# A Perceiver block on one core: key unit between first scores and values, feed-forward by two batches, self-attention norms batch by batch

## The chip, the core and the metric

The kernel runs on one core of one Trainium2 chip. The core has five engines with instruction streams of their own: TensorE (PE, matrix products), VectorE (DVE), ScalarE (ACT), GpSimd (POOL) and SyncE (SP, which issues most transfers). ACT and POOL issue transfers as well. [...] The metric is the device time of one execution in microseconds; the time of the kernel before is the median of three runs.

## What is computed

The block takes `x` (8 batches of 128 rows of 512) and a context (8 batches of 2048 rows of 384). All of it is float32, except where the feed-forward rounds.

```python
# 1. cross-attention over the context, 8 heads of 64
q = layernorm(x) @ Wq;  k = context @ Wk;  v = context @ Wv
x = x + softmax(q k^T / 8) v @ Wo + bo
# 2. masked self-attention; its input is n = layernorm(x)
n = layernorm(x)
logits = (n Wq + bq)(n Wk + bk)^T, -inf above the diagonal
x = x + n + (softmax(logits, axis=1) / sqrt(512)) @ (n Wv + bv)
# 3. feed-forward, 2048 hidden columns; n = layernorm(x)
h = quantize_e4m3(relu(n @ w1.T + b1))
x = x + quantize_e5m10(h @ quantize_e4m3(w2).T + quantize_e5m10(b2))
```

`layernorm` has no scale and no shift. `quantize` rounds to a small float format; the kernel does it with five DVE instructions.

## The kernel before, in words

**Order of the work.** The order on PE is that of the program text from beginning to end (`manual_schedule` of PE). The order on ACT and DVE is also that of the text, until the first quarter of the last batch is done (`in_turn.close()`, `first.close()`); from there a scheduler orders them by what is ready. POOL and SP are ordered by the scheduler throughout. Seven of the eight PSUM banks are handed round under the tag `bank`; the eighth holds the attention output `po`.

**Cross-attention.** For each batch b and each quarter m (two heads), the main loop (L721 to L780) issues, in this order on PE: `scores(b, m)` (16 products, L476), `attend` of the quarter before (64 products, L521), and a *unit* that prepares later data: `v_proj(b, 1)` in m = 0, `v_proj(b+1, 0)` in m = 1, `k_proj(b+1, m-2)` in m = 2 and 3. For the last batch the units are the self-attention's projections of rows 0 to 3. Between parts of the unit the other engines do the softmax of the quarter: DVE takes the maxes while copying the scores to `p` (L480, L486, L488), ACT takes the exponentials in two halves (`exps`, L494), DVE turns 32 x 32 blocks in place (`turns`, L507), and SP stores sixteen pieces of `p` into `pT` (L510), which `attend` of the next quarter reads. `p` and `pT` have one buffer each, so a quarter's maxes can start only when the quarter before has landed in `pT`.

**Units.** `k_proj` and `v_proj` use `block_product`: twenty products of sums of blocks in place of twenty-four, into seven banks, with `take` (a copy on ACT, L300) and `with_bank` or `less_bank` (additions on DVE, L303, L306) between. A bank that PE writes again must have been read before. The sums of the context's blocks are made by POOL (`sum_half`, L205), for the first batch by DVE. A unit is a generator: `first_of` issues it up to its next `yield` (after the first `take`, and after the fifth), `all_of` issues the rest. The first key unit is a plain product (`k_plain`, L353 to L366) over half the context; the other half of batch 0's keys is `k_proj(0, f2, (1,))`.

**Start.** `EARLY` products of an identity run before the first data are there. Then follow `k_plain(0)`, `q_norm(0)`, `k_plain(1)`, the transposes of the normed queries (`q_turn`), the query projection (`q_proj`), whose result goes to DRAM and is read back per batch (`load_q`), `k_proj(0, 0, (1,))`, `v_proj(0, 0)`, and `k_proj(0, 1, (1,))` before the loop. A one-element Exp (`warm`) makes ACT load its Exp table.

**Between cross-attention and self-attention.** In m = 0 of batch b, the output of batch b-1 is normalized and projected (`project`, L559 to L564: eight products, an addition on DVE into `xs[b]`, and for b up to 5 a store of the rows to DRAM, `xr`, from SP). In m = 0 of the last batch `bring_rows` (L566) reads rows 0 to 5 back, POOL issuing; `enter_self_attention` loads the three weights `swq`, `swk`, `swv` on POOL's queue; and rows 0 to 3 are normed and turned: statistics and subtraction on DVE (L111 to L118), Sqrt on ACT (L115), four transposes on PE (L131), a copy on ACT (L132), and `xs = xs + xn` on POOL (L124), each for one row block of 128. Rows 4 to 6 are normed by `sa1.norm` before the last `attend`, and turned after the last `project`; row 7 is normed and turned last.

**Feed-forward.** `hidden` (L824 to L838) makes the hidden columns for four batches at once: a product has 512 columns of four batches; two blocks of 128 hidden columns are rounded together. `output` (L841) has 16 products for one batch, `finish` (L849) adds the bias, rounds, adds the rows on POOL and stores. The last four batches' outputs stand behind the last hidden block.

Of the kernel before, what the change touches and what calls it, by code (L numbers as in the profile page):

```python
# [17 lines left out]
P = 128  # L18
# [29 lines left out]
def tile_perceiver_block(  # L48
# [34 lines left out]
    NG = 2  # L83
    TMPB = 2
    BK = 256
    EARLY = 9
    GB = B // NG
    GT = GB * S
    RSK = float(D) ** -0.5
# [264 lines left out]
    def k_plain(f2):  # L354


        k_tile(0, f2)
        pss = {(j, n): bank(f"k_{f2}_{j}_{n}") for j in range(2) for n in range(2)}
        for n, k in ((0, 0), (0, 1), (0, 2), (1, 0), (1, 1), (1, 2)):
            for j in range(2):  # L360
                nc.tensor.matmul(  # L361
                    pss[j, n], wk4[:, k, f2, j, :], xraw[0, 0][:, k, 2 * n : 2 * n + 2],
                    start=(k == 0), stop=(k == NKC - 1),
                )
        for (j, n), ps in pss.items():
            nc.scalar.copy(kts[0, f2][:, j, ts(n, 512)], ps)  # L366

    def k_proj(b, f2, halves=(0, 1)):

# [182 lines left out]
    def load_x(b):  # L552
        xs[b] = xp.tile([P, D], F32, tag="x", name=f"x_{b}")
        nc.sync.dma_start(xs[b], xd[:, b, :])

    def project(b, ot):
# [27 lines left out]
    class SelfAttention:  # L584


        def __init__(self, g, pool, w):
            self.g, self.pool = g, pool
            self.swq, self.swk, self.swv, self.bq, self.bk, self.bv, self.mask = w
            self.rows = [g * GB + i for i in range(GB)]  # L590
            self.xt = pool.tile([P, NK, GT], F32, tag="xt", name=f"xt_{g}")
            self.xn, self.es, self.vals = {}, {}, None

        def norm(self, b):
# [17 lines left out]
                    yield  # L612

        def queries(self):
            all_of(self.turned_rows("q", self.swq, self.bq))

        def keys(self):
            all_of(self.turned_rows("k", self.swk, self.bk))

        def weights(self, b):  # L620

            i = b % GB
            ps = bank(f"pl_{b}")
            for k in range(NK):
                nc.tensor.matmul(
                    ps[:, :S], self.kt[:, k, ts(i, S)], self.qt[:, k, ts(i, S)],
                    start=(k == 0), stop=(k == NK - 1),
                )
            lg = self.pool.tile([P, S], F32, tag="lg", name=f"lg_{b}", bufs=2)
            nc.vector.tensor_tensor(lg, ps[:, :S], self.mask, ALU.add)  # L630
            nm = small.tile([P, 1], F32, tag="snm", name=f"snm_{b}", bufs=4)
            nc.vector.reduce_max(nm, lg, axis=AX.X, negate=True)
            e = self.pool.tile([P, S], F32, tag="e", name=f"e_{b}", bufs=4)
            den = small.tile([P, 1], F32, tag="sden", name=f"sden_{b}", bufs=4)
            nc.scalar.activation(e, lg, AF.Exp, bias=nm, accum_out=den)
            r = small.tile([P, 1], F32, tag="sr", name=f"sr_{b}", bufs=4)
            nc.vector.reciprocal(r, den)
            nc.vector.tensor_scalar(e, e, r, RSK, ALU.mult, ALU.mult)
            self.es[b] = e

        def values(self, b):
            if self.vals is None:

                self.vals = self.pool.tile([P, GB, D], F32, tag="sk", name=f"sv_{self.g}")
            ps = bank(f"psv_{b}")
            for k in range(NK):
                nc.tensor.matmul(  # L647
                    ps, self.xt[:, k, ts(b % GB, S)], self.swv[:, k, :],
                    start=(k == 0), stop=(k == NK - 1),
                )  # L650
            nc.vector.tensor_tensor(self.vals[:, b % GB, :], ps, self.bv, ALU.add)

        def read(self, b):
            ps = bank(f"pr_{b}")
# [17 lines left out]
    def enter_self_attention():  # L672
        src.close()
        wsa = ctx.enter_context(tc.tile_pool(name="wsa", bufs=1, reuse_waits="tile"))
        sap = ctx.enter_context(tc.tile_pool(name="sap", bufs=1, reuse_waits="tile"))
        w = [
            load_w(wsa, a, NK, n, nc.gpsimd)
            for a, n in ((sa_wq, "swq"), (sa_wk, "swk"), (sa_wv, "swv"))
        ]
        w += [load_columns(wsa, sa_bq, "bq"), load_columns(wsa, sa_bk, "bk")]  # L680
        w.append(load_row(wsa, sa_bv, "bv"))

        mask = wsa.tile([P, P], F32, tag="mask", name="mask")
# [6 lines left out]
        return sap, w  # L690
# [25 lines left out]

# [4 lines left out]
    for b in range(B):  # L721
        last = b + 1 == B
        for m in range(NK):
# [11 lines left out]
            elif not last:  # L735
                unit = k_proj(b + 1, m - 2)
            elif m == 1:
                unit = sa0.turned_rows("q", sa0.swq, sa0.bq)
            elif m == 2:
                unit = sa0.turned_rows("k", sa0.swk, sa0.bk)  # L740
            else:
                for r in sa0.rows:
                    sa0.weights(r)
            if b == m == 0:

                first_of(unit)
                first_of(unit)
            exps(b, m, 0)
            if unit and not b == m == 0:
                first_of(unit)  # L750
            exps(b, m, 1)
            if m == 0 and b > 0:
                turned = normalized_first(b - 1)
                if last:
# [10 lines left out]
            if m == 0:  # L765
# [24 lines left out]
    xa.close()  # L790
    project(B - 1, ot)
    sa1.norm(sa1.rows[-1])
    for r in sa1.rows[:-1]:
        sa1.turn(r)
    for r in sa0.rows[2:]:
        sa0.read(r)
    sa1.turn(sa1.rows[-1])
# [21 lines left out]
            turned_into(xt, b, normed(b, sap, "xn", GB, "f"), "f")  # L819
        return xt  # L820

    hqs = {}

    def hidden(g, xt, blocks):  # L824
        if g not in hqs:
            hqs[g] = tp.tile([P, NHC, GT], BF16, tag="hq", name=f"hq_{g}", bufs=2)
        for c in blocks:
            h = tp.tile([P, 2, GT], F32, tag="h", name=f"h_{g}_{c}")
            for i in range(2):
                ps = bank(f"ph_{g}_{c + i}")  # L830
# [5 lines left out]
                nc.scalar.activation(  # L836
                    h[:, i, :], ps, AF.Relu, bias=b1c[:, c + i : c + i + 1]
                )  # L838
            quantize(nc, tp, hqs[g][:, c : c + 2, :], h, E4M3, "qh")

    def output(b, ps, blocks, cols=slice(0, D)):  # L841
        g, i = b // GB, b % GB
        for c in blocks:
            nc.tensor.matmul(  # L844
                ps[:, cols], hqs[g][:, c, ts(i, S)], w2[:, c, cols],
                start=(c == 0), stop=(c == NHC - 1),
            )

# [32 lines left out]
    for i in range(2):  # L881
# [58 lines left out]
```

## Time and profile before

| what | us |
|---|---|
| median of three runs | 1136.22 |
| lowest and highest run | 1134.65, 1136.40 |
| profiled execution, its time | 1134.23 |
| profiled execution, its span | 1132.5 |
| mean granted TensorE clock in it | 0.994 of full speed |
| DVE, ACT and POOL busy | 825.2, 329.4, 232.0 |

The profile is of one execution. "Busy" is the time in which an engine had an instruction under way. A line such as `PE pq L444 <- ACT xq L132: 1.0, 1, 1.0` in the list of waits says that PE, with the instruction of line 444 that writes tile `pq`, sat for 1.0 us until ACT had finished line 132's `xq`, once, the longest time 1.0. In the chain that ended last, each row has a start, a length, the engine, the tile, the line, and the number of instructions (x16). In a timeline row, the text behind the arrow `<-` of tile names tells what an instruction reads, and the bracket tells how long the engine idled before it and what ended that. `PEld` is the loading of weights, which runs beside PE. `SPq`, `ACTq` and `POOLq` are the issuing of transfers on an engine's queue. A stretch of the table by stretches gives start and end, their difference, then busy time and number of instructions of PE, PEld, DVE, ACT and POOL.

### The profile page before, as it was taken

Reading aid. Unit: us, or ns where it says so; the run is one execution under the profiler, and the core shown is the slowest. Engines: PE = TensorE matmul, PEld = TensorE weight load, DVE = VectorE, ACT = ScalarE, POOL = GpSimd, SP = SyncE. Lnnn points to the kernel's source line nnn. Section 1 sums busy time; section 2 is a strip of 40 time slices with the busy share of each in tenths; the row PEclk is TensorE's granted clock in tenths of the full one; section 3 lists DMA queues with packets and bytes.
Section 4 is the critical chain, followed back from the end, with each engine's and each line's share of the span. In section 5 each row is a group of like instructions: output and inputs, shape, how many; then the busy total and the mean of one; then the engine's idle time right before and its main releaser. Section 6 shows DMA issues by size and latency. Waiting matters only on the chain.

```text
span 1132.5 us, 16240 instructions
## 1 busy us (share of the span) xinstructions
PE 1110.0 (98%) x6034; PEld 787.3 (70%) x6034; DVE 825.2 (73%) x1705; ACT 329.4 (29%) x499; POOL 232.0 (20%) x322
## 2 busy tenths in 40 slices
PE   9999999999999999999999999999999999999996
PEld 5486787778878887777888788877865544444443
DVE  4946777676767776777777768767795559766867
ACT  3233222223323322222333232222342322222010
POOL 0304400540251044005303600440030000000101
PEclk9999999999999999999999999999999999999998
DMA  8412644643554465455335544653393473000001
GB/s 287 170 54 65 164 103 99 166 104 85 130 149 91 108 152 145 94 127 153 85 84 143 137 102 104 149 141 75 81 264 75 94 248 106 9 0 1 28 9 38
DMA packets 48495, 125.09 MB, mean 110 GB/s; under 512 B 10384, under 2 KB 15520, under 8 KB 47520
## 3 DMA queue, kind: packets, MB, share of 16 engines
q1 hardware_dynamic: 46192, 117.48, 40.1%
q0 software_dynamic: 1360, 5.78, 1.7%
q8 instruction: 48, 0.79, 0.3%
q10 hardware_dynamic: 864, 0.79, 0.2%
q14 instruction: 31, 0.25, 0.1%
HBM read 49.03 MB, written 7.86 MB: 50 GB/s over the span
## 4 chain that ended last, share of the span: by engine, by line
PE 94%; DVE 3%; DMA 2%; ACT 1%; issue 0%; SPq 0%; POOL 0%; DVEq 0%; ACTq 0%; POOLq 0%
PE pv_z L400 20%; PE pk_z L377 19%; PE po L521 10%; PE sc L476 10%; PE ph L832 10%; PE pk_b L377 3%; PE pv_b L400 3%; PE psq L606 2%; PE pq L444 2%; PE psk L606 2%; PE psv L647 2%; PE pf L844 2%; PE py L559 2%; PE k L361 2%; DMA pT<-p 2%; DVE p L507 1%
## 5 line engine op out<-in xcount | busy, mean ns | idle before, releaser
L494 ACT ACTIVATE p<-p,nm 128x2048 f32<-128x2048 f32 x64 | 128.1, 2002 | 430.9 <-DVE nm L488 331.1
L507 DVE STREAM_TRANSPOSE p<-p 128x512 f32<-128x512 f32 x256 | 158.9, 679 | 85.1 <-ACT p L494 84.9
L480 DVE TENSOR_SCALAR_CACHE_REDUCE p<-sc 128x512 f32<-128x512 f32 x256 | 159.0, 686 | 30.5 <-PE sc L476 28.8
L400 PE MATMUL pv_z<-wv_sums,x 128*128 128x256 f32 x640 | 158.9, 383 | 0.8 <-ACT v L300 0.8
L205 POOL TENSOR_TENSOR m<-x 128x256 f32<-128x256 f32 x70 | 51.3, 733 | 521.7 <-DMA x<-in_ctx_t_dram 458.5
L377 PE MATMUL pk_z<-x,wk_sums 128*128 128x256 f32 x600 | 149.4, 382 | 0.4 <-DVE kt L306 0.4
L400 PEld LDWEIGHTS pv_z<-wv_sums,x 128*128 128x128 f32 x640 | 121.0, 191 | 20.5 <-issue 1.9
L521 PEld LDWEIGHTS po<-pT,v 128*64 128x64 f32 x2048 | 112.8, 138 | 24.3 <-issue 22.0
L377 PEld LDWEIGHTS pk_z<-x,wk_sums 128*128 128x128 f32 x600 | 112.7, 190 | 18.5 <-issue 2.9
L476 PE MATMUL sc<-kt,q 64*128 64x512 f32 x512 | 119.6, 602 | 2.5 <-DVE p L480 2.5
L521 PE MATMUL po<-pT,v 128*64 128x128 f32 x2048 | 120.5, 276 | 0.0
L400 PE MATMUL pv_z<-wv_sums,m 128*128 128x256 f32 x448 | 108.6, 382 | 2.6 <-DVE v L303 2.4
L832 PE MATMUL ph<-xf,w 128*128 128x512 f32 x256 | 110.4, 592 | 0.0
L377 PE MATMUL pk_z<-m,wk_sums 128*128 128x256 f32 x420 | 101.9, 380 | 0.7 <-ACT kt L300 0.7
L400 PEld LDWEIGHTS pv_z<-wv_sums,m 128*128 128x128 f32 x448 | 83.6, 191 | 16.1 <-DVE v L303 2.8
L832 PEld LDWEIGHTS ph<-xf,w 128*128 128x128 f32 x256 | 48.6, 190 | 60.4 <-issue 59.8
L476 PEld LDWEIGHTS sc<-kt,q 64*128 64x128 f32 x512 | 47.3, 186 | 62.2 <-issue 53.5
L377 PEld LDWEIGHTS pk_z<-m,wk_sums 128*128 128x128 f32 x420 | 78.9, 190 | 13.2 <-ACT kt L300 1.1
L300 ACT COPY v<-pv_z 128x512 f32<-128x512 f32 x112 | 62.8, 589 | 60.6 <-PE pv_z L400 60.1
L300 ACT COPY kt<-pk_z 128x512 f32<-128x512 f32 (+1 forms) x112 | 59.8, 559 | 55.0 <-PE pk_z L377 54.6
L205 POOL TENSOR_TENSOR x<-x 128x256 f32<-128x256 f32 x98 | 70.4, 737 | 0.9 <-DMA x<-in_ctx_t_dram 0.9
L303 DVE TENSOR_TENSOR v<-pv_z,v 128x512 f32<-128x512 f32 x96 | 63.2, 685 | 5.4 <-PE pv_z L400 5.3
(171 smaller groups left out, 1213.2 us busy)
## 6 DMA issues: line engine op xcount, KB each, us to landing
pT<-p SPq DMA_DIRECT2D x512, 128.0 KB, 2.4
x<-in_ctx_t_dram SPq DMA_DIRECT2D x45, 512.0 KB, 5.4
w<-in_w_t_dram SPq DMA_DIRECT2D x1, 4096.0 KB, 12.5
w2f<-in_w_t_dram SPq DMA_DIRECT2D x16, 256.0 KB, 2.7
x_in<-in_x_dram SPq DMA_DIRECT2D x8, 256.0 KB, 6.9
xd<-x_in SPq DMA_DIRECT2D x2, 1024.0 KB, 4.2
qd<-xq SPq DMA_DIRECT2D x8, 256.0 KB, 3.2
q<-qd SPq DMA_DIRECT2D x8, 256.0 KB, 3.2
```

The costliest lines, as they stand in the source:

```text
L205: eng.tensor_tensor(x_block(b, h, to), x_block(b, h, one), x_block(b, h, two), ALU.add if op == "+" else ALU.subtract,)
L300: nc.scalar.copy(outs[ij], views(ps))
L303: nc.vector.tensor_tensor(outs[to], views(ps), outs[other], op)
L377: nc.tensor.matmul(ps[:, ts(i, BK)], wk_sums[:, WSLOT[WAT[r]], f2, :], x_block(b, h, XAT[r]), start=start and i == 0, stop=True, skip_grou ...
L400: nc.tensor.matmul(ps[:, ts(t, 256)], x[:, ts(t, P)], wv_sums[:, WSLOT[WAT[r]], :], start=start and t == 0, stop=True, skip_group_check=True,)
L476: nc.tensor.matmul(pair[i], q[r, :], kts[b, m // 2][r, m % 2, ts(n, 512)], start=True, stop=True)
L480: nc.vector.tensor_scalar(p[:, :, i].rearrange("p g (t i) -> p t g i", i=SQ)[:, ts(n, Q)], pair[i].rearrange("p (t g i) -> p t g i", g=Q, ...
L494: nc.scalar.activation(p[:, :, i], p[:, :, i], AF.Exp, bias=nms[b, m][:, i : i + 1], scale=SCALE, accum_out=sums[b][:, h : h + 1],)
L507: nc.vector.transpose(p[:, g, i], p[:, g, i])
L521: nc.tensor.matmul(pos[b][h * DH : (h + 1) * DH, ts(m, P)].rearrange("p (a i) -> p a i", a=Q), v[:, jt % 8, ts(2 * m + h, DH)], turned_[b, ...
L606: nc.tensor.matmul(ps, weight[:, k, ts(m, P)], self.xt[:, k, :], start=(k == 0), stop=(k == NK - 1),)
L832: nc.tensor.matmul(ps, w1[:, k, ts(c + i, P)], xt[:, k, :], start=(k == 0), stop=(k == NK - 1),)
```

## The change

Six things are changed.

1. `EARLY` goes from 9 to 7.
2. `k_plain` copies each pair of products when it is done, and is a generator with a break after two thirds of its products; `q_turn(0)` stands in the break of `k_plain(1)`. The one-element Exp moves from before `k_proj(0, 0, (1,))` into the query projection.
3. `k_proj(0, 1, (1,))` moves from before the loop into b = m = 0, between `scores(0, 0)` and `v_proj(0, 1)`. The Exp of the first half stands before its last part.
4. Rows 0 to 5 are normed in the loop: `row_stats(b-1)` at the end of m = 0, `norm_rows(b-1)` in m = 1 behind the second Exp. The normed and turned rows go to a new DRAM tensor `xtd`, ACT issuing; the sums `x + n` go to `xr`, POOL issuing. ACT's order in m = 1 is thus: Exp, copy of the turned rows, issue of the store, `take` copies of the unit. The self-attention's `xt` is read from `xtd` on POOL's queue, for rows 0 to 3 ahead of the three weights; rows 6 and 7 are normed and turned as before.
5. The feed-forward's hidden part takes two batches at a time (256 columns), with four hidden blocks rounded together (two at the very end).
6. The outputs of a pair of batches stand in the middle of the next pair's hidden blocks, so that two batches' outputs are left behind the last hidden block.

```diff
-    EARLY = 9
+    EARLY = 7
...
         k_tile(0, f2)
-        pss = {(j, n): bank(f"k_{f2}_{j}_{n}") for j in range(2) for n in range(2)}
-        for n, k in ((0, 0), (0, 1), (0, 2), (1, 0), (1, 1), (1, 2)):
+        for n in range(2):
+            pss = [bank(f"k_{f2}_{j}_{n}") for j in range(2)]
+            for k in range(NKC):
+                for j in range(2):
+                    nc.tensor.matmul(
+                        pss[j], wk4[:, k, f2, j, :], xraw[0, 0][:, k, 2 * n : 2 * n + 2],
+                        start=(k == 0), stop=(k == NKC - 1),
+                    )
+                if (n, k) == (1, 0):
+                    yield
             for j in range(2):
-                nc.tensor.matmul(
-                    pss[j, n], wk4[:, k, f2, j, :], xraw[0, 0][:, k, 2 * n : 2 * n + 2],
-                    start=(k == 0), stop=(k == NKC - 1),
-                )
-        for (j, n), ps in pss.items():
-            nc.scalar.copy(kts[0, f2][:, j, ts(n, 512)], ps)
+                nc.scalar.copy(kts[0, f2][:, j, ts(n, 512)], pss[j])
...
         nc.vector.tensor_tensor(xs[b], ps, xs[b], ALU.add)
-        if b < B - 2:
-            nc.sync.dma_start(xr[:, b, :], xs[b])
+
+    def row_stats(b):
+        st = small.tile([P, 6], F32, tag="st", name=f"st_s_{b}", bufs=4)
+        nc.vector.bn_stats(st, xs[b])
+        mv = small.tile([P, 2], F32, tag="mv", name=f"mv_s_{b}", bufs=4)
+        nc.vector.bn_aggr(mv, st)
+        sd = small.tile([P, 1], F32, tag="sd", name=f"sd_s_{b}", bufs=4)
+        nc.scalar.activation(sd, mv[:, 1:2], AF.Sqrt, bias=eps)
+
+        nc.scalar.activation(warm, eps, AF.Exp)
+        stats[b] = mv, sd
+
+    def norm_rows(b):
+
+        mv, sd = stats[b]
+        rs = small.tile([P, 1], F32, tag="rs", name=f"rs_s_{b}", bufs=4)
+        nc.vector.reciprocal(rs, sd)
+        xn = tmp.tile([P, D], F32, tag="t", name=f"xn_s_{b}")
+        nc.vector.tensor_scalar(xn, xs[b], mv[:, 0:1], rs, ALU.subtract, ALU.mult)
+        nc.gpsimd.tensor_tensor(xs[b], xs[b], xn, ALU.add)
+        nc.gpsimd.dma_start(xr[:, b, :], xs[b])
+        pt = bank(f"pt_s_{b}")
+        for k in range(NK):
+            nc.tensor.transpose(pt[:, ts(k, P)], xn[:, ts(k, P)], ident)
+        xt = tmp.tile([P, NK, S], F32, tag="t", name=f"xt_s_{b}")
+        nc.scalar.copy(xt, pt.rearrange("p (k t) -> p k t", k=NK))
+        nc.scalar.dma_start(xtd[:, :, ts(b, S)], xt)
...
             self.xt = pool.tile([P, NK, GT], F32, tag="xt", name=f"xt_{g}")
+            there = slice(g * GT, min((g + 1) * GT, (B - 2) * S))
+            nc.gpsimd.dma_start(self.xt[:, :, : there.stop - there.start], xtd[:, :, there])
...
-        w = [
-            load_w(wsa, a, NK, n, nc.gpsimd)
-            for a, n in ((sa_wq, "swq"), (sa_wk, "swk"), (sa_wv, "swv"))
-        ]
+        w = [wsa.tile([P, NK, D], F32, tag=n, name=n) for n in ("swq", "swk", "swv")]
+        sa0 = SelfAttention(0, sap, w)
+        for t, a in zip(w, (sa_wq, sa_wk, sa_wv)):
+            nc.gpsimd.dma_start(t, a.rearrange("(k p) n -> p k n", p=P))
...
-    k_plain(0)
+    all_of(k_plain(0))
     both = [q_norm(0)]
-    k_plain(1)
+    rest = first_of(k_plain(1))
     qds = [q_turn(0, both[0])]
     both.append(q_norm(1))
+    all_of(rest)
     q_proj(0, both[0], qds[0], range(2))
     qds.append(q_turn(1, both[1]))
+
+    warm = small.tile([P, 1], F32, tag="warm", name="warm")
+    nc.scalar.activation(warm, eps, AF.Exp)
     q_proj(0, both[0], qds[0], range(2, NK))
...
-    warm = small.tile([P, 1], F32, tag="warm", name="warm")
-    nc.scalar.activation(warm, eps, AF.Exp)
     all_of(k_proj(0, 0, (1,)))
     all_of(v_proj(0, 0))
     next_half(1, 0)
-    all_of(k_proj(0, 1, (1,)))
...
             if b == m == 0:
-                first_of(unit)
-                first_of(unit)
-            exps(b, m, 0)
-            if unit and not b == m == 0:
-                first_of(unit)
+                keys = k_proj(0, 1, (1,))
+                first_of(keys)
+                first_of(keys)
+                exps(b, m, 0)
+                all_of(keys)
+            else:
+                exps(b, m, 0)
+                if unit:
+                    first_of(unit)
             exps(b, m, 1)
+            if m == 1 and 0 < b and not last:
+                norm_rows(b - 1)
...
-                    sap, w = enter_self_attention()
-                    sa0 = SelfAttention(0, sap, w)
-                    for r in sa0.rows:
-                        sa0.norm(r)
-                        sa0.turn(r)
+                    sap, w, sa0 = enter_self_attention()
+                elif b > 0:
+                    row_stats(b - 1)
     for r in sa0.rows:
         sa0.values(r)
     sa1 = SelfAttention(1, sap, w)
-    for r in sa1.rows[:-1]:
-        sa1.norm(r)
+    sa1.norm(B - 2)
...
-    for r in sa1.rows[:-1]:
-        sa1.turn(r)
+    sa1.turn(B - 2)
...
-    def hidden(g, xt, blocks):
-        if g not in hqs:
-            hqs[g] = tp.tile([P, NHC, GT], BF16, tag="hq", name=f"hq_{g}", bufs=2)
+    def hidden(batches, xt, blocks):
+
+        n, b0 = len(batches) * S, batches[0]
...
+        per = blocks.step
...
-                        ps, w1[:, k, ts(c + i, P)], xt[:, k, :],
+                        ps[:, :n], w1[:, k, ts(c, P)], xt[:, k, at],
...
-    half = NHC // 2
-    hidden(0, xf0, range(0, half, 2))
-    xf1 = normed_rows(1, "sq")
-    hidden(0, xf0, range(half, NHC, 2))
-    hidden(1, xf1, range(0, 4, 2))
-    for b in range(GB):
-        ps = bank(f"pf_{b}")
-        output(b, ps, range(NHC))
-        finish(b, ps)
-    hidden(1, xf1, range(4, NHC, 2))
-
-    pair = [bank(f"pf_{b}") for b in range(GB, GB + 2)]
-    for i in range(2):
-        output(GB + i, pair[i], range(NHC - 2))
-    for i in range(2):
-        output(GB + i, pair[i], range(NHC - 2, NHC))
-        finish(GB + i, pair[i])
+    half, xfs = NHC // 2, [xf0]
+    pairs = [range(b, b + 2) for b in range(0, B, 2)]
+    hidden(pairs[0], xf0, range(0, NHC, 4))
+    for i in range(1, len(pairs)):
+        last = i + 1 == len(pairs)
+        if i == 1:
+            xfs.append(normed_rows(1, "sq"))
+        hidden(pairs[i], xfs[i // 2], range(0, half, 4))
+        for b in pairs[i - 1]:
+            ps = bank(f"pf_{b}")
+            output(b, ps, range(NHC))
+            finish(b, ps)
+        hidden(pairs[i], xfs[i // 2], range(half, NHC - 4 if last else NHC, 4))
+    hidden(pairs[-1], xfs[1], range(NHC - 4, NHC, 2))
```

More of the change, by code (lines that the diff above doesn't have):

```diff
@@ L554, in load_x @@
         nc.sync.dma_start(xs[b], xd[:, b, :])
+    xtd = dram.tile([P, NK, B * S], F32, tag="xtd", name="xtd")
+    stats = {}
     def project(b, ot):
@@ L588, in __init__ @@
             self.g, self.pool = g, pool
-            self.swq, self.swk, self.swv, self.bq, self.bk, self.bv, self.mask = w
+            self.w = w
             self.rows = [g * GB + i for i in range(GB)]
             self.xt = pool.tile([P, NK, GT], F32, tag="xt", name=f"xt_{g}")
+            there = slice(g * GT, min((g + 1) * GT, (B - 2) * S))
+            nc.gpsimd.dma_start(self.xt[:, :, : there.stop - there.start], xtd[:, :, there])
             self.xn, self.es, self.vals = {}, {}, None
@@ L614, in queries @@
         def queries(self):
-            all_of(self.turned_rows("q", self.swq, self.bq))
+            all_of(self.turned_rows("q", self.w[0], self.w[3]))
         def keys(self):
-            all_of(self.turned_rows("k", self.swk, self.bk))
+            all_of(self.turned_rows("k", self.w[1], self.w[4]))
         def weights(self, b):
@@ L629, in weights @@
             lg = self.pool.tile([P, S], F32, tag="lg", name=f"lg_{b}", bufs=2)
-            nc.vector.tensor_tensor(lg, ps[:, :S], self.mask, ALU.add)
+            nc.vector.tensor_tensor(lg, ps[:, :S], self.w[6], ALU.add)
             nm = small.tile([P, 1], F32, tag="snm", name=f"snm_{b}", bufs=4)
@@ L647, in values @@
                 nc.tensor.matmul(
-                    ps, self.xt[:, k, ts(b % GB, S)], self.swv[:, k, :],
+                    ps, self.xt[:, k, ts(b % GB, S)], self.w[2][:, k, :],
                     start=(k == 0), stop=(k == NK - 1),
                 )
-            nc.vector.tensor_tensor(self.vals[:, b % GB, :], ps, self.bv, ALU.add)
+            nc.vector.tensor_tensor(self.vals[:, b % GB, :], ps, self.w[5], ALU.add)
         def read(self, b):
@@ L689, in enter_self_attention @@
         w.append(mask)
-        return sap, w
-    k_plain(0)
+        return sap, w, sa0
+    all_of(k_plain(0))
     both = [q_norm(0)]
-    k_plain(1)
+    rest = first_of(k_plain(1))
     qds = [q_turn(0, both[0])]
     both.append(q_norm(1))
+    all_of(rest)
     q_proj(0, both[0], qds[0], range(2))
     qds.append(q_turn(1, both[1]))
+    warm = small.tile([P, 1], F32, tag="warm", name="warm")
+    nc.scalar.activation(warm, eps, AF.Exp)
     q_proj(0, both[0], qds[0], range(2, NK))
@@ L737, in tile_perceiver_block @@
             elif m == 1:
-                unit = sa0.turned_rows("q", sa0.swq, sa0.bq)
+                unit = sa0.turned_rows("q", sa0.w[0], sa0.w[3])
             elif m == 2:
-                unit = sa0.turned_rows("k", sa0.swk, sa0.bk)
+                unit = sa0.turned_rows("k", sa0.w[1], sa0.w[4])
             else:
@@ L820, in normed_rows @@
         return xt
-    hqs = {}
-    def hidden(g, xt, blocks):
-        if g not in hqs:
-            hqs[g] = tp.tile([P, NHC, GT], BF16, tag="hq", name=f"hq_{g}", bufs=2)
-        for c in blocks:
-            h = tp.tile([P, 2, GT], F32, tag="h", name=f"h_{g}_{c}")
-            for i in range(2):
-                ps = bank(f"ph_{g}_{c + i}")
+    hqs, firsts = {}, {}
+    def hidden(batches, xt, blocks):
+        n, b0 = len(batches) * S, batches[0]
+        if b0 not in firsts:
+            t = tp.tile([P, NHC, n], BF16, tag=f"hq{n}", name=f"hq_{b0}", bufs=3)
+            firsts[b0] = t
+            for i, b in enumerate(batches):
+                hqs[b] = t[:, :, ts(i, S)]
+        at = slice(b0 % GB * S, b0 % GB * S + n)
+        per = blocks.step
+        for c0 in blocks:
+            h = tp.tile([P, per, n], F32, tag="h", name=f"h_{b0}_{c0}")
+            for i in range(per):
+                c = c0 + i
+                ps = bank(f"ph_{b0}_{c}")
                 for k in range(NK):
                     nc.tensor.matmul(
-                        ps, w1[:, k, ts(c + i, P)], xt[:, k, :],
+                        ps[:, :n], w1[:, k, ts(c, P)], xt[:, k, at],
                         start=(k == 0), stop=(k == NK - 1),
                     )
[L836 to L839, printed above, removed]
+                nc.scalar.activation(h[:, i, :], ps[:, :n], AF.Relu, bias=b1c[:, c : c + 1])
+            quantize(nc, tp, firsts[b0][:, c0 : c0 + per, :], h, E4M3, "qh")
     def output(b, ps, blocks, cols=slice(0, D)):
-        g, i = b // GB, b % GB
         for c in blocks:
             nc.tensor.matmul(
-                ps[:, cols], hqs[g][:, c, ts(i, S)], w2[:, c, cols],
+                ps[:, cols], hqs[b][:, c, :], w2[:, c, cols],
                 start=(c == 0), stop=(c == NHC - 1),
@@ L866, in tile_perceiver_block @@
     quantize_w2()
-    half = NHC // 2
-    hidden(0, xf0, range(0, half, 2))
-    xf1 = normed_rows(1, "sq")
-    hidden(0, xf0, range(half, NHC, 2))
-    hidden(1, xf1, range(0, 4, 2))
-    for b in range(GB):
-        ps = bank(f"pf_{b}")
-        output(b, ps, range(NHC))
-        finish(b, ps)
-    hidden(1, xf1, range(4, NHC, 2))
-    pair = [bank(f"pf_{b}") for b in range(GB, GB + 2)]
-    for i in range(2):
-        output(GB + i, pair[i], range(NHC - 2))
-    for i in range(2):
-        output(GB + i, pair[i], range(NHC - 2, NHC))
-        finish(GB + i, pair[i])
+    half, xfs = NHC // 2, [xf0]
[12 more added lines that the diff above has]
+    hidden(pairs[-1], xfs[1], range(NHC - 4, NHC, 2))
     ps = bank(f"pf_{B - 2}")
```

## The prediction

> **What bounds the kernel now.** I read the busy table first, then the waits of TensorE, the chain that ended last, and single stretches of the timeline. TensorE (PE) works for 98% of the span; no other engine is near it.
>
> ```profile
> PE 1110.0 (98%) x6034; PEld 787.3 (70%) x6034; DVE 825.2 (73%) x1705; ACT 329.4 (29%) x499; POOL 232.0 (20%) x322
> PE 94%; DVE 3%; DMA 2%; ACT 1%; issue 0%; SPq 0%; POOL 0%; DVEq 0%; ACTq 0%; POOLq 0%
> ```
>
> So the change can win only what PE idles or runs slowly, plus the ends. TensorE's waits (us, times, longest):
>
> ```profile
> PE sc L476 <- DVE p L480: 2.5, 1, 2.5
> PE pv_z L400 <- DVE v L303: 2.4, 1, 2.4
> PE pt_s L131 <- DVE xn_s L118: 1.8, 1, 1.8
> PE pq L444 <- ACT xq L132: 1.0, 1, 1.0
> PE pv_z L400 <- ACT v L300: 1.0, 2, 0.8
> ```
>
> They are single events. The third is row 7's norm at 930, which the change keeps. The chain places the first two (start, length): batch 7's second scores and batch 0's value projection.
>
> ```profile
> 95.10 3.63 PE sc L476 x16
> 98.73 6.25 PE pv_z L400 x28
> 105.49 2.10 ACT p L494 x2
> 107.62 4.86 DVE p L507 x8
> 114.50 4.54 PE pv_z L400 x12
> ...
> 840.21 7.44 DMA pT<-p
> 847.96 1.48 DVE xn_s L118
> 851.22 5.31 PE po L521 x64
> ```
>
> `po` takes 3.64 elsewhere in the chain, 5.31 here. Two stretches show why (columns: PE, weight loads, DVE, ACT and POOL busy, then granted clock, DMA share, GB/s):
>
> ```profile
> 112.00:119.00 7.00, 4.58 (x14) 3.68 (x14) 5.61 (x9) 0.00 (x0) 0.00 (x0) 0.76 0.93 205
> 848.00:856.00 8.00, 5.90 (x60) 5.15 (x62) 6.65 (x20) 2.39 (x2) 3.78 (x3) 0.79 0.01 2
> ```
>
> Each stall (2.42 and 2.46 us) is followed by half clock: the trace's clock records give 3.41 us at half, 114.60 to 118.02 and 851.88 to 855.29. Half of 3.41, 1.7 us, belongs to the price of each stall. A rule of the Trainium skill speaks against that: "TensorE: Matmul & The Clock Gate", Part 1: The HAM clock gate, lets the clock fall after about 3.4 us of idleness. By the rule these stalls would cost only their length, 3.4 us less in all; the rows decide, so I count both halves, and count the same price if a new stall of 2 us arises.
>
> **The change part by part.** Against the profiled execution (span 1132.5, time 1134.23).
>
> *Start, gain 2.6.* Copies come after each pair of key products, a query turn stands between them, and the Exp table load moves earlier. The three waits go: 1.0 before `pq` (with its gap 1.17), the early one in part (9 warm-up products become 7; 0.3), and 0.98 where the table load (1.28 on ACT) delays the copies of `k_proj(0,0)`. Sum 2.5 to 2.6. The early part has two ends: -0.3, or +1.7 if the full clock is granted a window later; the first half-speed products end at 5.37 and the first data had landed at 5.0, so I take -0.3.
>
> *`k_proj(0,1)` behind the first scores, gain 5.5.* Now: keys 9.6 (with short stalls), scores 3.63, values 22.9 up to `sc(0,1)` at 121.6 = 36.15. The values' PE work is 17.27 (as in the later units); the rest is 0.97 + 2.58 of stalls and 1.7 of half clock, as PE runs into `take` copies behind two Exp (105.49 on) and DVE's turns (107.62, 4.86). After: scores 3.63, keys 8.63, which cover Exp and turns, about 1.04 of stall (a copy behind the first Exp), values 17.27: 30.6. ACT, DVE and SP (16 pT stores) have about 2 us of slack: pT(0,0) lands 29.8 us after the start, its buffer's next use is at 31.8. Ends: 3.5 (the stall returns once) to 6.5.
>
> *Norms of rows 0 to 5 in the loop, cost 6.8.* For b = 1 to 6: at the end of m = 0 two statistics on DVE (0.62 + 0.1), a Sqrt and two table loads on ACT (2 x 1.28), in front of 7 us in which ACT waits for maxes: hidden. If the cover were gone, Exp, turns and pT would be 3 us late. At m = 1: reciprocal and xn (0.6 on DVE) under the wait for Exp; four transposes on PE (16 `pt_f` take 1.75, so 0.44), plain path: x6 = 2.62. On POOL an add (1.3) and a store's issue (0.7), behind the sums; nobody waits. SP loses its store (0.33 each). The ACT queue matters:
>
> ```profile
> 337.20 2.01 ACT L494 ACTIVATE p<-p,nm 128x2048 f32<-128x2048 f32 x1
> 339.11 0.19 ACT L494 ACTIVATION_READ_ACCUMULATOR p<-p,nm 128x1 f32 x1
> 339.20 1.56 ACT L300 COPY v<-pv_z 128x512 f32<-128x512 f32 x3
> 339.97 1.05 PE L400 MATMUL pv_z<-wv_sums,m 128*128 128x256 f32 x4
> ```
>
> The first of the three copies frees the bank that the product at 339.97 overwrites: no slack. After, between Exp and that copy stand the `xt` copy (0.5) and the store's issue. The store has 512-byte runs like `q<-qd`, which SP issues in 0.58 (median of its rows); with 0.15 until the copy is visible that is 1.2, and PE itself comes 0.44 later: 0.7 of stall, x6 = 4.2. Ends: 0 if ACT's queue runs on past the issue (-4.2), 1.1 each (6.6) if issue on ACT is slower than on SP. The Trainium skill ("DMA: Bandwidth & Descriptors", Issuing engines are not separate DMA queues) says that queues of several engines share the same DMA engines, and spreading over them saves only issue time: by it the move frees 0.33 on SP, where nothing waits, and pays 0.58 on ACT, where PE does. The rows agree in sign: I keep 0.7.
>
> *Batch 7, gain 4.1.* PE's part: 16 transposes go (1.75). `scores(7,1)` starts at 843.6 and lasts 3.63, but `po` starts only at 851.2: 3.9 of stall, in which DVE's xn waits for `rows` with the maxes behind it; 3.4 of it go (the rest below). With 1.7 of half clock: 6.9. `attend(7,1)` would be ready at 874.0 - 6.9 = 867.1 on PE. But row 6's norm now stands in front of the maxes of `scores(7,1)` on DVE (1.65, which holds their banks: the 0.5 left), and ACT needs a Sqrt and an Exp table (1.28). Scores now start at 843.6 - 1.75 = 841.8; in the loop pT lands 25.8 after (327.5 to 353.3): 867.6; with 1.65 it is 869.2, with all 870.5. I take 869.2: new stall 2.1, left 4.8; less 0.7 for another half-clock window at 40%: 4.1. SP has the pT stores alone. POOL's queue has changed order: rows, `xt_0` (1 MB, waits for the end of the values, 838.3), then swq, swk, swv. By the old latencies (`rows<-xr` 7.2, `swq` 10.9) swq lands near 847, used at 849.7; the others later, as used. Bounds: nothing, to 4 us late. Rows 4 and 5 at the end (8 transposes, 0.9) were under `py`'s chain to `psq` (922.4 to 932.0), which keeps row 7's norm: nothing.
>
> *Feed-forward by two batches, gain 1.7.* `ph` has 512 products of 256 columns for 256 of 512. Of the rows, 12 products of 256 (`pv_z`) take 2.59, so 512 x 0.2159 = 110.55; 96 of 512 take 41.20, so 256 x 0.4292 = 109.87: +0.68. The end is DVE's:
>
> ```profile
> 1108.01 12.12 PE pf L844 x64
> 1121.21 1.75 DVE qb_e L40 x2
> 1125.84 1.26 POOL L854 TENSOR_TENSOR y<-y,rows 128x512 f32<-128x512 f32 x1 [3.03 <-issue]
> 1126.16 1.22 DVE L854 TENSOR_TENSOR y<-y,rows 128x256 f32<-128x256 f32 x1
> 1129.19 0.43 DVE L854 TENSOR_TENSOR y<-y,rows 128x256 f32<-128x256 f32 x1
> ```
>
> Four finishes pile up: DVE ends 21.6 after the last `ph`. After, batches 4 and 5 are put out (2 x 3.45 = 6.9) and finished before it; behind the last `ph` remain 0.45 for its quantizing, 6.9 of products and some 5 of finishes. 0.68 + 6.9 + 12.3 = 19.9 against 21.6: 1.7 (0 to 3).
>
> Sum: -2.6 - 5.5 + 6.8 - 4.1 - 1.7 = -7.1: 1127.1 for the profiled execution. It lies 2.0 below the median of the three runs (1136.22, from 1134.65), so on that scale 1129.1, 0.6% faster. Of that scatter, 0.2% or 2.3 us is what the measurement can tell.
>
> **The rivals.** *Full gain.* The ACT issue hides, and batch 7 has no new stall: 4.2 + 2.1 + 0.7 more, 1122. For it: an issue need not hold up ACT's next instruction; no row shows one in front of work there. Against: by the lines above the copy has no slack. Chance 0.15.
>
> *POOL's queue is late at batch 7.* Behind `xt_0` the weights land 4 late in front of `psq` (used at 849.7, 2.7 after the landing I work with; `swk` once took 17.0) and the clock halves for a window: 4 + 1.7 = 5.7 given back, 1135. Chance 0.12, slightly faster or the same.
>
> *Slower: ACT's store holds PE.* It decides from a stall of 0.7 + 7.1/6 = 1.9 us in each unit, that is an issue of 0.58 + 1.2 = 1.8 on ACT in place of 0.58. With an issue of 2.2 the stall is 2.3: 9.6 more than I count, 1138.7. It is then also near the 2.4 after which the trace twice shows half clock: six times 1.7 on top would make 1149. For it: POOL issues last 0.93 (`swv`), pT lands in 4.2 to 10 us under traffic (chain, 828.93). Against: ACT's six issues at the start (`w_in<-in_xa_wk_dram`, 1 KB runs) last 0.33 to 0.46 each, no longer than SP's beside them. Chance 0.15.
>
> **How the numbers follow.** Likeliest (0.58): 1129, own range 1125 to 1133. Faster: 0.58 x 0.97 + 0.15 + half of 0.12 = 0.77; same 0.08; slower 0.15. Range 1121 to 1139: the full gain below, the slower case's mild end above.
>
> **What would show it.** Start: `scores(0,1)` near 113.4, and full clock from 100 to 120. Loop: six waits of `pv_z` for ACT's `v`, about 0.7 each, and 0.44 of `pt_s`; a batch (102.87 now, 327.48 to 430.35) takes about 104.0; under 103.5 the ACT queue hid its store, over 105 the slower rival is at work. Batch 7: `attend(7,1)` near 874.0 - 8.1 + 6.8 - 4.8 = 867.9, after a wait for pT of about 2. End: DVE's last instruction about 20 after the last `ph`. The forecast is wrong in its core if PE's gaps in front of 120 are still 2 or more, or if swq lands after its use.

## The result, and the profile after

The changed kernel takes 1164.45 us (median of four, 1162.61 to 1166.07) against 1135.58 for the kernel before on the same chip: ratio 1.0255, 95% interval 1.024 to 1.027. The forecast was 1129, with a range from 1121 to 1139. The profiled execution took 1164.29, its span 1162.4, with a mean clock of 0.983 (0.994 before): 29.9 more span.

The busy table and the shares of the chain, after:

```profile
PE 1127.2 (97%) x6286; PEld 844.8 (73%) x6286; DVE 826.4 (71%) x1710; ACT 355.1 (31%) x549; POOL 237.2 (20%) x330
PE 82%; DVE 5%; POOL 4%; DMA 3%; SPq 3%; ACT 2%; issue 1%; ACTq 0%; DVEq 0%
```

PE is still busy for 97%, but its share of the chain fell from 94% to 82%, and POOL and SP's queue appear in it with 4% and 3%, where they had none. The waits of PE, after:

```profile
PE sc L479 <- DVE p L483: 15.7, 4, 4.1
PE pv_z L403 <- POOL x L205: 3.0, 4, 1.0
PE pt_s L131 <- DVE rs_f L117: 2.8, 1, 2.8
PE po L524 <- issue: 1.6, 1, 1.6
...
PE pv_z L403 <- ACT v L300: 1.1, 2, 0.6
```

The old single waits at the start and at batch 7 are gone. New is a wait of scores for DVE's maxes that comes four times. Four is the hint, since the norms run in six batches. To find the place, I took from both traces the start of each of the 32 score groups; the distance to the next one is the length of a quarter:

| quarter | before | after | times |
|---|---|---|---|
| start of scores(0,1) | 121.57 | 114.78 | once |
| m = 1, b = 1 to 6 | 24.76 | 26.10 to 26.57 | 6 |
| m = 2, b = 1 to 4 | 24.74 | 31.97, 32.29, 33.00, 33.06 | 4 |
| m = 2, b = 5 and 6 | 24.74 | 24.74 | 2 |
| b = 7, m = 0, 1, 2 | 30.80, 26.46, 21.21 | 28.62, 22.14, 22.88 | once |
| scores(7,3) to first `ph` | 91.0 | 93.9 | once |
| first `ph` to the end | 149.9 | 148.2 | once |

In sums: -6.9 at the start (0.1 of it behind scores(0,1)), +9.0 in the six m = 1, +31.4 in the four m = 2, -4.8 in batch 7, +2.9 in the self-attention's second half, -1.7 in the feed-forward: +29.9, all of it. The four quarters of m = 2 are the result. Batches 1 to 4 have what 5 and 6 lack: a `load_x` for the next batch, which SP issues during m = 1. SP's queue in batch 1, before and then after:

```profile
221.25 1.28 SPq L166 DMA_DIRECT2D x<-in_ctx_t_dram  x3
225.37 0.33 SPq L564 DMA_DIRECT2D xr<-x  x1
228.64 0.33 SPq L554 DMA_DIRECT2D x<-xd  x1
237.25 10.03 SPq L510 DMA_DIRECT2D pT<-p  x16
```

```profile
214.35 1.28 SPq L166 DMA_DIRECT2D x<-in_ctx_t_dram  x3
237.48 0.33 SPq L557 DMA_DIRECT2D x<-xd  x1
238.03 10.65 SPq L513 DMA_DIRECT2D pT<-p  x16
```

`x<-xd` is `load_x` (of batch 2, put early by the scheduler). It fills one of two row buffers, and may start when the old content has been stored. Before, SP itself stored it at 225.37, and the load went out 8.6 us ahead of the first pT store. After, the content is free only when POOL has done the block sums in front of it, the addition, and the store. POOL's timeline, after:

```profile
232.71 0.74 POOL L205 TENSOR_TENSOR x<-x 128x256 f32<-128x256 f32 x1
233.39 1.29 POOL L589 TENSOR_TENSOR x<-x,xn_s 128x512 f32<-128x512 f32 x1
234.99 0.69 POOL L590 DMA_DIRECT2D xr<-x  x1 [0.31 <-POOL x L589]
```

The store lands at 237.43, SP's load goes out at 237.48, and the sixteen pT stores stand behind it, though their data were turned by 232.2. SP's own waits in these stretches of batch 1 name the transfer, before and then after:

```profile
SPq L554 <- DMA xr<-x: 2.9, 1, 2.9
```

```profile
SPq L557 <- DMA xr<-x: 21.8, 1, 21.8
```

The last pT store lands at 250.5. `p` has one buffer, so DVE cannot start the next maxes, PE runs out of banks for the scores, and half clock follows (the stretch's columns as in the prediction):

```profile
250.66 0.69 DVE L483 TENSOR_SCALAR_CACHE_REDUCE p<-sc 128x512 f32<-128x512 f32 x1 [6.05 <-DMA pT<-p]
```

```profile
243.80:256.00 12.20, 8.30 (x41) 4.54 (x42) 5.96 (x19) 0.00 (x0) 0.00 (x0) 0.72 0.48 104
```

In this batch PE waits 3.9, and the trace's clock records then give 6.8 us at half (249.20 to 256.03), which cost another 3.4. The other three batches have the same 6.8. So of the 31.4 some 15.7 are waiting and some 13.7 are half clock.

### The profile page after: what moved, and what is told of

It is laid out like the page before. It is cut to its first block, busy times and chain, and to the rows that moved or that the text cites. A ratio compares the mean times of both kernels' runs of the same rounds, so it can differ in the third digit from the quotient of the medians.

```text
span 1162.4 us, 16819 instructions
## 1 busy us (share of the span) xinstructions
PE 1127.2 (97%) x6286; PEld 844.8 (73%) x6286; DVE 826.4 (71%) x1710; ACT 355.1 (31%) x549; POOL 237.2 (20%) x330
## 4 chain that ended last, share of the span: by engine, by line
PE 82%; DVE 5%; POOL 4%; DMA 3%; SPq 3%; ACT 2%; issue 1%; ACTq 0%; DVEq 0%
PE pk_z L380 19%; PE pv_z L403 17%; PE ph L876 9%; PE po L524 8%; PE sc L479 7%; PE pv_b L403 3%; PE pk_b L380 3%; SPq L513 2%; PE psk L640 2%; PE psv L681 2%; PE pq L447 2%; POOL m L205 2%; PE k L362 2%; DMA x<-in_ctx_t_dram 2%; PE pf L885 2%; POOL x L205 2%
## 5 line engine op out<-in xcount | busy, mean ns | idle before, releaser
L483 DVE TENSOR_SCALAR_CACHE_REDUCE p<-sc 128x512 f32<-128x512 f32 x256 | 159.0, 686 | 50.8 <-DMA pT<-p 25.4
L479 PE MATMUL sc<-kt,q 64*128 64x512 f32 x512 | 128.8, 612 | 15.7 <-DVE p L483 15.7
L524 PEld LDWEIGHTS po<-pT,v 128*64 128x64 f32 x2048 | 118.6, 144 | 28.9 <-issue 27.3
L524 PE MATMUL po<-pT,v 128*64 128x128 f32 x2048 | 126.3, 284 | 1.6 <-issue 1.6
L380 PEld LDWEIGHTS pk_z<-x,wk_sums 128*128 128x128 f32 x600 | 112.7, 190 | 19.8 <-issue 2.7
L876 PE MATMUL ph<-xf,w 128*128 128x256 f32 x512 | 111.3, 379 | 0.0
L479 PEld LDWEIGHTS sc<-kt,q 64*128 64x128 f32 x512 | 50.1, 188 | 79.3 <-issue 54.9
L876 PEld LDWEIGHTS ph<-xf,w 128*128 128x128 f32 x512 | 97.3, 190 | 13.8 <-issue 0.5
L303 DVE TENSOR_TENSOR v<-pv_b,v 128x512 f32<-128x512 f32 x48 | 33.1, 689 | 49.4 <-PE pv_b L403 49.4
```

Of the source, the lines that this page charges most:

```text
L303: nc.vector.tensor_tensor(outs[to], views(ps), outs[other], op)
L380: nc.tensor.matmul(ps[:, ts(i, BK)], wk_sums[:, WSLOT[WAT[r]], f2, :], x_block(b, h, XAT[r]), start=start and i == 0, stop=True, skip_grou ...
L479: nc.tensor.matmul(pair[i], q[r, :], kts[b, m // 2][r, m % 2, ts(n, 512)], start=True, stop=True)
L483: nc.vector.tensor_scalar(p[:, :, i].rearrange("p g (t i) -> p t g i", i=SQ)[:, ts(n, Q)], pair[i].rearrange("p (t g i) -> p t g i", g=Q, ...
L524: nc.tensor.matmul(pos[b][h * DH : (h + 1) * DH, ts(m, P)].rearrange("p (a i) -> p a i", a=Q), v[:, jt % 8, ts(2 * m + h, DH)], turned_[b, ...
L876: nc.tensor.matmul(ps[:, :n], w1[:, k, ts(c, P)], xt[:, k, at], start=(k == 0), stop=(k == NK - 1),)
```

## The experiments

**1. Load the rows on POOL's queue.** The only change to the changed kernel:

```diff
-        nc.sync.dma_start(xs[b], xd[:, b, :])
+        nc.gpsimd.dma_start(xs[b], xd[:, b, :])
```

> The changed kernel with one line other: the rows of the residual (load_x, 256 KB per batch) are loaded on POOL's queue in place of SP's. Theory A (head of SP's queue): in batches 1 to 4 SP stands at load_x of the next batch, which waits until the row buffer is free, and that now comes after POOL's block sums, the addition and POOL's store; the sixteen pT stores of m = 1 stand behind it. Then the four long periods of m = 2 (31.97, 32.29, 33.00, 33.06 where the others last 24.74) go back to 24.7: 31.4 us less, near 1133. m = 1 stays at 26.1 to 26.6. Rival B (traffic: the two new stores slow the landing of pT) or rival C (the store on ACT's queue delays Exp, turns and so pT): the four periods stay over 31, time 1155 or more.

Measured: 1132.59 (20 runs), ratio 0.9981 to before, interval 0.9974 to 0.9988. m = 2 is 24.74 in five of the six batches and 24.95 in one. SP's queue in batch 1:

```profile
214.18 1.28 SPq L166 DMA_DIRECT2D x<-in_ctx_t_dram  x3
230.92 10.56 SPq L513 DMA_DIRECT2D pT<-p  x16
```

The pT stores go out 7.1 earlier. No other line was touched: the two new stores are still there, one of them on ACT's queue. Traffic and ACT's queue are not the cause of the long quarters. One line of queue choice is worth about 31 us (1.0255 against 0.9981 of before).

**2. Take the store of the turned rows off ACT's queue**, with `load_x` left on SP.

```diff
-        nc.scalar.dma_start(xtd[:, :, ts(b, S)], xt)
+        nc.sync.dma_start(xtd[:, :, ts(b, S)], xt)
```

> The changed kernel with the store of the turned rows (xtd) issued on SP in place of ACT; load_x stays on SP, ahead of it. Theory A: the four long periods of m = 2 stay at 31 to 33, since the wait of load_x is untouched; m = 1 becomes shorter by 0.7 each (25.4 to 25.8), as the copy behind the second Exp is no longer held: 1158 to 1163. Rival C (ACT's queue is the cause): the long periods go, 1133 or less. Rival B (traffic): no change, 1164.

Measured: 1165.11, ratio 1.0269, 1.0251 to 1.0288. m = 1 fell to 25.4 to 25.8, as expected, but the whole time did not fall to 1158 to 1163: the long quarters stayed and grew, to 34.75, 34.78, 32.82 and 33.72. They begin 0.3 to 0.8 earlier, and this store is one thing more between `load_x` and pT on SP: counted from the start of m = 1, the first pT store goes out 0.5 to 0.8 later, in batch 2 even 2.6. By the time alone this could pass for rival B's "no change"; it is experiment 1 that excludes B. My slower rival, ACT's queue, is ruled out as the main cause. The price of ACT's store is seen in m = 1: 26.26 on average in the changed kernel, 25.57 here, where only this store's queue is other. That is 0.7 per batch. ACT's timeline in batch 1 of the changed kernel shows how it comes about:

```profile
229.59 0.57 ACT L595 COPY xt_s<-pt_s 128x512 f32<-128x512 f32 x1
230.20 0.59 ACTq L596 DMA_DIRECT2D xtd<-xt_s  x1
230.83 1.56 ACT L300 COPY v<-pv_z 128x512 f32<-128x512 f32 x3 [0.66 <-ACT xt_s L595]
```

The three `take` copies start after the issue. The list of waits names POOL for most of PE's waits here; with the store off ACT, that row falls from 3.0 to 0.3 though POOL's work is the same, so it was ACT.

**3. The start alone**, on the kernel before: items 1 to 3 of the change.

```diff
-    EARLY = 9
+    EARLY = 7
...
+    rest = first_of(k_plain(1))
...
+                keys = k_proj(0, 1, (1,))
+                first_of(keys)
+                first_of(keys)
+                exps(b, m, 0)
+                all_of(keys)
```

> The kernel before with the changes of the start alone (EARLY 7, copies and query turn inside the key products, Exp table load earlier, second key unit behind the first scores). In the changed kernel the second scores start 6.8 us earlier than before. If the parts add up, 1135.6 - 6.8 = 1128.8. If a later part takes it back (a clock window, a transfer that is not ahead), 1131 or more.

Measured: 1128.28, ratio 0.994, 0.9926 to 0.9955. The start is a gain by itself.

**4. The norms alone**, on the kernel before: item 4 of the change.

```diff
+            if m == 1 and 0 < b and not last:
+                norm_rows(b - 1)
...
+                elif b > 0:
+                    row_stats(b - 1)
```

> The kernel before with the norms of rows 0 to 5 inside the loop alone (start and feed-forward as before). Theory A by the changed trace: +31.4 (four periods of m = 2) + 9.0 (six of m = 1) - 4.8 (last batch) + 2.9 (end of self-attention) = +38.5: 1174. If the start's shift of the block sums against the norms matters (the norms alone do not bring the wait), 1145 or less.

Measured: 1172.99, ratio 1.0337, 1.0322 to 1.0353. The long quarters are 31.98, 32.75, 32.51 and 32.59. The parts add up; the loss does not need the start's changes.

**5. Free the buffer earlier** in place of moving the load: the addition on DVE, its store on SP, `load_x` as in the change.

```diff
-        nc.gpsimd.tensor_tensor(xs[b], xs[b], xn, ALU.add)
-        nc.gpsimd.dma_start(xr[:, b, :], xs[b])
+        nc.vector.tensor_tensor(xs[b], xs[b], xn, ALU.add)
+        nc.sync.dma_start(xr[:, b, :], xs[b])
```

> The changed kernel with the addition x + n on DVE in place of POOL, and its store on SP in place of POOL; load_x keeps its place on SP between that store and the pT stores, xtd stays on ACT. Theory A (load_x waits for a row buffer that POOL frees late): the buffer is now free about 12.5 us after the scores' start in place of 19.8, before the first pT store is ready at about 14: the long periods of m = 2 shrink from 31-33 to 24.7-26, time 1132 to 1138. If it is enough that any store and load stand in front of pT on SP (order, not lateness), they stay over 30: 1160 or more.

Measured: 1132.55 (10 runs), ratio 0.9969, 0.996 to 0.9979. All six m = 2 last 24.74. SP's queue in batch 1, where scores(1,1) started 2.3 later than in the changed kernel:

```profile
229.42 0.33 SPq L590 DMA_DIRECT2D xr<-x  x1
231.47 0.33 SPq L557 DMA_DIRECT2D x<-xd  x1
232.85 11.53 SPq L513 DMA_DIRECT2D pT<-p  x16
```

Store and load stand in front of pT, as they did in the kernel before, and m = 2 loses nothing, because they are ready first. It is the lateness of what stands at the head of the queue, not the order.

This profile also shows the end of my bound on `EARLY` that I had not taken (+1.7). PE's first key products, in experiment 1's profile and in this one:

```profile
4.99 7.36 PE L362 MATMUL k<-x,w_in 128*128 128x512 f32 x15 [0.27 <-DMA w_in<-in_xa_wk_dram]
```

```profile
5.39 6.90 PE L362 MATMUL k<-x,w_in 128*128 128x512 f32 x9 [0.67 <-DMA w_in<-in_xa_wk_dram]
```

The identity products end at 4.7 in both. Where the weights landed 0.4 later, PE did 9 products in the time in which it else does 15, the trace's first record of full clock begins at 11.01 in place of 6.35, and scores(0,0) started at 86.1 in place of 83.6. That is one trace of each kernel.

**6. Both repairs**: `load_x` on POOL, `xtd` on SP (the diffs of 1 and 2).

> The changed kernel with load_x on POOL's queue and the xtd store on SP's: both repairs. By the two single repairs: the long m = 2 periods gone, m = 1 at 25.4 to 25.8 in place of 26.4 to 26.8, six times 1.0: 1132.6 - 6 = 1126.6. If the xtd store, which now stands ahead of pT on SP, delays pT, m = 2 grows by 0.5 or more and the time is 1130 or more.

Measured: 1133.18 (9 runs), ratio 0.998, 0.997 to 0.9989. I expected 1126.6 and named the other outcome, which came: m = 1 is 25.5 to 26.0, but m = 2 lasts 24.9 to 26.5, in sum 5.4 more. What m = 1 saved is lost again in m = 2. Its scores now come 0.8 earlier than in experiment 1, while pT lands 27.1 to 29.0 after the scores' start in place of 26.4 to 28.3. The store in front of pT is only part of this: it delays pT's first store by about 0.5, and experiment 7, which has no such store on SP, loses in m = 2 as well.

**7. Load and `xtd` store both on POOL.**

```diff
-        nc.scalar.dma_start(xtd[:, :, ts(b, S)], xt)
+        nc.gpsimd.dma_start(xtd[:, :, ts(b, S)], xt)
```

> The changed kernel with load_x and the xtd store on POOL's queue. Nothing of the norms stands on ACT's or SP's queue: m = 1 at 25.2 to 25.8, m = 2 at 24.7, time 1126 to 1127. If POOL's later block sums come too late behind the waiting load, PE waits for POOL in m = 3 or m = 0: 1130 or more.

Measured: 1130.46, ratio 0.9951, 0.9936 to 0.9966. m = 1 is 25.4 to 26.0, and m = 2 is 2.2 longer in sum. The waits in m = 3 and m = 0 that I had named for this time did not come. What slows the landing of pT here (26.5 to 28.4 after the scores' start; 24.5 to 25.8 in the kernel before) was not separated. It has the lowest median of the versions with norms in the loop, and is slower than experiment 8, the same kernel without them.

**8. Start and feed-forward, no norms in the loop.**

> The kernel before with the start and the feed-forward of the change, without the norms in the loop. Start alone gave 1128.3. From the first hidden product to the end the changed trace is 1.7 shorter than before (148.2 against 149.9): 1126.6. If the feed-forward's saving is lost elsewhere, 1128 or more.

Measured: 1125.88, ratio 0.9914, 0.9897 to 0.993. That is 0.7 below the 1126.6 expected.

**9 and 10. The last batch of that kernel, and `EARLY`.** In 9 only the order of the weights' loads is other; in 10 `EARLY` is 9.

```diff
-        w = [
-            load_w(wsa, a, NK, n, nc.gpsimd)
-            for a, n in ((sa_wq, "swq"), (sa_wk, "swk"), (sa_wv, "swv"))
-        ]
+        w = [wsa.tile([P, NK, D], F32, tag=n, name=n) for n in ("swq", "swk", "swv")]
+        for i in (0, 2, 1):
+            a = (sa_wq, sa_wk, sa_wv)[i]
+            nc.gpsimd.dma_start(w[i], a.rearrange("(k p) n -> p k n", p=P))
```

> The kernel of p_start_ffn with the three self-attention weights loaded in the order swq, swv, swk in place of swq, swk, swv (POOL's queue is in order, and swv waits for the end of the value products, so swk too now comes after it). In p_start_ffn the pT stores of the last batch's first quarter take 5 to 9 us each (2.4 elsewhere) beside rows (2 MB), swq and swk (1 MB each), landing at 837.1; scores(7,1) wait 2.5 for it, with half clock behind. If it is this traffic, pT(7,0) lands 2 to 5 us earlier and the wait goes: 1125.9 - 2.5 to - 4.2 = 1121.7 to 1123.4. If DVE's norms of rows 0 to 3 in front of the maxes are the cause: no change, 1125.9. If swk is late, a wait before psk: 1127 or more.

> The kernel of p_start_ffn with EARLY back at 9. In the e3_sum_dve profile, with 7, the key weights landed at 5.39, PE idled 0.67 before the first key product and then ran at half clock for a window: its second key unit's scores came 2.5 us later than in the other profiles with 7. With 9 the identity products reach to 5.4: if 7 saves 0.3 to 0.5 when data come at 4.8 to 5.0 and loses 2.5 now and then, the two medians are alike, 1125.5 to 1126.5, and the highest run with 9 is not above 1127.5.

Measured: 9 took 1126.99, ratio 0.9923 (0.9911 to 0.9936); 10 took 1125.6, ratio 0.9914 (0.9901 to 0.9928). So 9 brought none of the gain that I had counted. In 9, pT(7,0) lands at 834.7 in place of 837.1, though its stores go out 0.8 later: the traffic did slow it. Yet PE's wait grew, from 2.5 to 3.2:

```profile
PE sc L479 <- DVE p L483: 3.2, 1, 3.2
```

DVE starts its first max at 843.6, behind the subtractions of the norms, so the landing alone was not what decided. The expectation also took half clock behind the wait of 2.5 in kernel 8; that trace has none. In 10 the time is that of 8 within the runs' scatter: a smaller `EARLY` brings nothing that can be measured.

**11 and 12. Norms of rows 0 to 3 behind scores(7,1) and its `attend`**, on kernel 10; in 12 with the order of loads of 9 too.

```diff
-                    for r in sa0.rows:
-                        sa0.norm(r)
-                        sa0.turn(r)
...
             elif m == 1:
+                for r in sa0.rows:
+                    sa0.norm(r)
+                    sa0.turn(r)
                 unit = sa0.turned_rows("q", sa0.swq, sa0.bq)
```

> The kernel of p_start_ffn_e9 with the norms and turns of rows 0 to 3 placed in the program behind scores(7,1) and attend(7,0), in front of the query unit. b_swk_last took the traffic away from pT(7,0), but scores(7,1) still waited (3.2 for DVE's maxes): DVE's norms of later rows stand in front of the maxes. Here DVE has row 4's subtraction behind the maxes. If these norms are what scores(7,1) wait for, the wait of 2.5 and its half clock (1.7) shrink: 1121.5 to 1124. If pT's late landing alone decides, 1125.6.

> As b_norm_after, with the weights loaded in the order swq, swv, swk too: norms behind the scores and pT(7,0) landing about 3 earlier. If both hold the maxes in turn, this one gains what either alone does not: 1121 to 1122.5 (wait and half clock gone); if the norms alone do, as b_norm_after; if neither, 1125.6.

Measured: 11 took 1125.59, ratio 0.9921 (0.9906 to 0.9936); 12 took 1124.02, ratio 0.9905 (0.9889 to 0.9922). Neither interval stands clear of those of 8 and 10. The waits of PE in 11 and then in 12:

```profile
PE psq L609 <- ACT xt L132: 1.6, 2, 0.9
...
PE sc L479 <- DVE p L483: 1.2, 1, 1.2
```

```profile
PE psq L609 <- ACT xt L132: 2.8, 2, 2.1
```

With both, the wait of scores is gone, and in its place `psq` waits for the turned rows, which ACT copies behind an Exp. From scores(7,0) to scores(7,3) it is 77.3 in 8, 78.5 in 10, 78.3 in 11, 76.4 in 12. One wait took the other's place: the rows above sum to 2.8 in both. What sets 12 apart from 10 and 11 is half clock: 10 and 11 have 3.4 us of it behind the wait, 8 and 12 have none. Number 12 has the lowest median here, but that it beats 8 and 10 is not shown.

## Why the prediction was wrong

**The step that failed** is in the part on the norms in the loop: "On POOL an add (1.3) and a store's issue (0.7), behind the sums; nobody waits." Somebody does: the row buffer that this store reads has a next user, `load_x`, and that stands on SP in front of the pT stores. I had listed that SP loses its store, and took it for a relief of 0.33; in truth the store's move to POOL made the buffer free 15.7 us later: its store landed 19.8 after the start of scores(1,1) (217.6 to 237.4), SP's had landed 4.1 after it (224.5 to 228.6). Missing term: 7.2 to 8.3, four times, 31.4. Experiments 1 and 5 take it away by two different means, 4 shows it without the other parts.

**The slower rival** had the right sign for a wrong reason. It put the loss on ACT's queue in m = 1, with an issue that lasts 1.8 or more. The issue lasted 0.52 to 0.59; my 0.58 from SP's rows was right.

**The start** was forecast at 8.1 and gave 6.8 (scores(0,1) at 114.8 for 113.4). The stalls went as said. Most of what is missing lies in the first key products, which take 21.7 in place of 20.6. With `EARLY` at 7 they started 0.6 earlier, but the first record of full clock begins at 6.86 where it began at 5.38, and that takes 0.7 back.

**m = 1** was forecast at 1.1 more per batch and was 1.5 more. Both terms of the forecast were right: the transposes take 0.44, and ACT's store costs 0.7 (26.26 against 25.57, experiment 2). From the Exp's end to the first `take` copy it is 1.24 (229.59 to 230.83) for the 1.2 forecast, though the hand-over from the copy to the issue takes 0.04, not the 0.15 that I put in. What was missing are the statistics, which were not hidden. I had set them against ACT's idle time, but they stand on DVE between the addition of `py` and the maxes. The maxes end 7.0 after the scores' start where they ended 6.1, in all six batches, and the second Exp starts 9.95 to 10.43 after it in place of 9.79. On average that is 0.3 per batch. (In experiment 1 the second Exp starts at 10.2 to 10.5, and m = 1 is 26.58 on average; why it is later there was not looked into.)

**Batch 7** was forecast at 4.1, or 4.8 without half clock behind the new stall, and gave 4.8: the new stall is 1.6 for 2.1, and no half clock follows it. The order on POOL's queue did no harm. Part of this is luck. The forecast counted 1.7 for the half clock behind the old stall, as if each such stall brought it. Experiments 3 and 8 have the same work there and the same wait, 2.46 and 2.45, at full clock; against their batch 7 the gain is 4.2 and 3.7. The explanation, too, was only half of it: experiment 9 shows that an earlier landing of pT alone does not free the maxes there, 11 that a later place of the norms alone frees them in part, and only 12, with both, has no wait of the scores.

**The feed-forward** was forecast at 1.7 and gave 1.7 (149.9 to 148.2). DVE ends 12.4 after the last `ph`, as the 12.3 of the sum has it; the "about 20" given as a sign to look for took in what stands before that product.

**The self-attention's second half**, costed at nothing, lost 2.9. The wait for row 7's norm is 2.8 for 1.8, but that is the place of the eight transposes that went, as I had said. The loss is half clock, from 959.17 to 966.00: `psq` takes 16.4 for 14.0 and the four transposes in front of it 0.4 more. Whether the norms bring it is not shown: the last section has such a loss in experiment 3, without them.

With the four waits away, as in experiment 1, the kernel stands at 0.9981 of before: the gains of the start and of the feed-forward are eaten by the norms. The norms in the loop cost more in six batches than they bring in the last, also when they are queued well: 1130.5 in experiment 7 against 1125.9 in experiment 8.

## What to carry to other kernels

When a store moves to another queue, follow the buffer that it reads to its next user, and look at what stands behind that user in its own queue: a load that waits holds everything behind it, and pays the price of the busiest thing there. A count is a good detective: six batches had the new work, four had the loss, and only one instruction occurs in just those four. And a new step on an engine with much idle time is only hidden if nothing on the path to the next wait stands behind it.

## What the runs showed of the hardware

**The same wait can cost nothing but its length, or halve the clock behind it.** The same pair of waits, 1.78 and 0.68 us, stands in front of `psq` in the kernel before and in the start alone (experiment 3), with the same instructions around it. The stretches from 920 to 944 of the first and from 914 to 936 of the second:

```profile
920.00:944.00 24.00, 21.54 (x66) 10.43 (x65) 20.01 (x49) 7.44 (x14) 1.26 (x1) 1.00 0.65 244
```

```profile
914.00:936.00 22.00, 19.54 (x51) 9.03 (x50) 19.35 (x48) 6.17 (x12) 1.26 (x1) 0.84 0.65 258
```

One keeps full clock, the other has half clock from 922.99 to 929.82, and `psq` takes 14.0 in the one and 17.1 in the other. Kernels 8 and 10, which differ in `EARLY` alone, have the same two waits again (1.78 and 0.67): 8 has half clock for 3.4 us and takes 15.7, 10 has none and takes 14.0. At scores(7,1) it is the other way round: both wait 2.45, and there 10 has 3.4 us of half clock and 8 none. The instructions around these waits are the same, and only where in time they fall is other; what decides is not shown. So a wait of about 2.5 us in these traces has a price of 2.5, 4.2 or 5.5, and which one a change brings can't be read from its length.

**SP has eight transfers in flight here, and the program sets that.** In the last batch of kernel 8, with stores that take 7 to 9 us, SP issues eight of them 0.6 apart (818.6 to 823.0) and the ninth at 825.69, just after the first has landed at 825.62. This is not shown to be a limit of the queue: in the trace the instruction before the ninth store waits for the semaphore (103) that the first store raises when it lands, and the eight semaphores 100 to 107 serve SP's transfers in turn. From the ninth store on, SP runs at the pace of the landings.
